# Attention pieces with two stacked parts, the key's exchanged form by transfers in SBUF, scores as two 32-row products a head

## Chip, cores and metric

One core of a Trainium2 chip runs the whole program in one launch. The metric is the device time of that launch in microseconds. Three runs of the kernel before were timed; a further execution was profiled.

## The reference

The program is one block of a network on 4 batches of 256 tokens with 512 features: attention with 32 heads of 16 features and a small adapter, a feed layer with a selection, a state-space mixer, and the feed layer again. Only the attention is touched. Cut to it:

```python
qkv = jnp.einsum('btc,oc->bto', x, w_attn)                 # x: (4, 256, 512), normed
q, k, v = split into heads: (4, 32, 256, 16)
q = _apply_rope(q, cos, sin); k = _apply_rope(k, cos, sin)
scores = jnp.einsum('bhqd,bhkd->bhqk', q, k) / sqrt(16)
scores = jnp.where(causal, scores, -inf)
y = jnp.einsum('bhqk,bhkd->bhqd', softmax(scores), v)
# adapter: 10 extra keys and values, the same for all batches
ascores = gating * softmax(jnp.einsum('bhqd,xhkd->bhqk', q, ak) / sqrt(512))
y = y + jnp.einsum('bhqk,xhkd->bhqd', ascores, av)
out = jnp.einsum('btc,oc->bto', y, w_proj)
```

## The kernel before

All numbers are float32. [...]

**Units.** The attention loop has 32 passes, i = 0 to 31; pass i handles four heads `u = i % 8` of batch `b = i // 8`. In what follows a pass is a unit. The order of TensorE's instructions in the loop is the order of the program (`manual_schedule` for that engine); the order on the other engines and queues is made by the framework's planner from its own cost estimates.

**Rows.** `prepared` makes for each batch and each half c of its 256 tokens the rotated queries (f = 0) and keys (f = 1), 128 tokens by 32 heads by 16 features, `qk[b, c, f]`. GpSimd adds the two halves of the rotation at L329.

**Pieces.** A piece covers eight heads, so two units: `pieces(b, q, f)`. `stacked` (L347, L348, GpSimd) writes each head's 16 features four times side by side, as upper and lower parts: for queries the parts stand as upper, upper, lower, nothing (cleared once at L338), for keys as upper, lower, upper. One cast writes the two upper copies (128x256), one subtraction the lower part (128x128). Then TensorE turns four blocks of 128 columns for each half c (L442, tile `trp`, two PSUM banks), and ScalarE copies each bank into the piece `pc0` or `pc1` (L444). Now a head stands in 64 rows, two heads to a block of 128 rows.

**When.** `pieces` runs in two steps: GpSimd's part at the end of unit i, TensorE's and ScalarE's part in unit i + 1. Queries are turned in even units, keys in odd ones; the unit after the keys' turn (an even one) is the first to use that piece of keys. The queries' piece is one unit earlier still. The first piece of queries and of keys is made before the loop.

**Scores.** `scores(b, u)` multiplies, for each half c of the queries, each of four heads' 64 rows by the keys' 64 rows (L488): for c = 1 against all 256 keys, for c = 0 against the first 128. Heads in rows 0 to 63 and 64 to 127 go to two PSUM banks, pool `a_s` with three. VectorE adds the causal mask and takes the maximum (L499), ScalarE takes the exponential (L511). The products for c = 1 stand at the start of a unit, those for c = 0 after the unit's long products (the projections `pq` of the next batch, `po` or the feed layer).

**The rest of a unit**, in TensorE's order: scores for c = 1; on even units `adapter_scores` (`pa`, L452, from a query piece and the adapter's keys `akbd`); the turn of a piece (`trp`); the long products; scores for c = 0; the weighted sums of the unit two before (`py`, L538 and L544); the turn of the exponentials of the unit before (`ptr`, L528, copied by ScalarE and VectorE at L529); the turn of the sums (`try`, L558); on even units the turn of the adapter's scores (`tra`, L460); sometimes turns of other tiles. All these PSUM tiles but scores and `py` share the pool `a_m` with four banks. In units 28 to 31 and behind the loop the feed layer's products `pd` use two of these banks at a time until VectorE and ScalarE have chosen from them.

**The adapter's keys.** `adapter_weights` multiplies the 10 extra keys, repeated eight times, and masks them (`bdk`) so that 20 rows hold two heads side by side; `adapter_keys` stacks and turns them into `akbd` (L378, L381), in unit 1.

**Loads.** `load` is a transfer issued by SyncE (SP). In the loop SP issues the projection's weights (L297, asked for in unit 3) and, from unit 23 on, the feed layer's (L199); both wait for GpSimd to free their buffers.

Of the kernel before, what the change touches and what calls it, by code (L numbers as in the profile page):

```python
# [9 lines left out]
F32 = mybir.dt.float32  # L10
F32R = mybir.dt.float32r
# [3 lines left out]
AF = mybir.ActivationFunctionType  # L15
ALU = mybir.AluOpType
# [4 lines left out]
P = 128  # L21
B, L, C = 4, 256, 512
# [4 lines left out]
NH, HD = 32, 16  # L27
NA = 10
# [11 lines left out]
COLS = {}  # L40
_at = 0
for _name, _w in (
    ("ident", 128), ("neg", 256), ("rot", 128), ("bdk", 2), ("bdv", 128), ("idx", 1), ("tri", 256),
):
    COLS[_name] = (_at, _at + _w)
    _at += _w
# [5 lines left out]
def constants():  # L52

    c = np.zeros((P, NCOL), np.float32)

    def put(name, v):
        c[: v.shape[0], COLS[name][0] : COLS[name][1]] = v

    r = np.arange(P)
    put("ident", np.eye(P, dtype=np.float32))  # L60
    put("tri", (np.arange(L)[None, :] >= r[:, None] % Q).astype(np.float32))
    put("neg", np.where(np.arange(L)[None, :] - P > r[:, None], -1e30, 0.0).astype(np.float32))
    theta = (
        np.float32(1.0)
        / np.float32(10000.0) ** (np.arange(0, HD, 2, dtype=np.float32) / np.float32(HD))
    ).astype(np.float32)
    angle = np.outer(np.arange(L, dtype=np.float32), theta).astype(np.float32)
    cos, sin = np.cos(angle), np.sin(angle)
    table = np.stack([np.concatenate([cos, cos], 1), np.concatenate([-sin, sin], 1)], 1)
    table = np.stack([table * np.float32(0.25), table], 1).astype(np.float32)  # L70

    put("rot", table.reshape(2, P, -1).transpose(1, 0, 2).reshape(P, -1))
    put("bdk", (r[:, None] // NA == np.arange(2)[None, :]).astype(np.float32))
    put("bdv", (np.arange(80)[:, None] // NA == r[None, :] // HD).astype(np.float32))
    put("idx", r[:, None].astype(np.float32))
    return c
# [3 lines left out]
def hybrid_kernel(  # L80
# [6 lines left out]
    nc = tc.nc  # L87
    load = nc.sync.dma_start
# [5 lines left out]
    con = keep.tile([P, NCOL_KEEP], F32R, name="con")  # L94
    ident = con.bitcast(F32)
# [3 lines left out]
    a_s = keep.tile([P, 1], F32, name="a_s")  # L99
# [172 lines left out]
    def attention(later, region):  # L272
        with ExitStack() as es:
            inner, banks = ExitStack(), ExitStack()
            pool = lambda name, bufs, **kw: es.enter_context(tc.tile_pool(name=name, bufs=bufs, **kw))
            w1 = pool("a_w", 1)
            p1 = pool("a1", 1)
            p2 = pool("a2", 2)
            p3 = pool("a3", 3)
            ps, ps_s, ps_y = (  # L280
                banks.enter_context(tc.tile_pool(name=name, bufs=bufs, space=PSUM))
                for name, bufs in (("a_m", 4), ("a_s", 3), ("a_y", 1))
            )

            acon = w1.tile([P, NCOL_ATTN - NCOL_KEEP], F32, name="acon")
# [46 lines left out]


            NS = 2
            stacks = [[w1.tile([P, 8, 4, HD], F32R, name=f"st{f}{i}") for i in range(NS)] for f in range(2)]
            for f in range(2):
                for v in stacks[f]:
                    nc.gpsimd.memset(v.bitcast(F32), 0.0)  # L338
            turn_at = [0, 0]
            HI = (slice(0, 2), slice(0, 3, 2))  # L340
            LO = (2, 1)

            def stacked(src, f, n=P):
                st = stacks[f][turn_at[f] % NS]
                turn_at[f] += 1
                v = src.unsqueeze(2)
                nc.gpsimd.tensor_copy(st[:n, :, HI[f], :], v.to_broadcast([n, 8, 2, HD]))  # L347
                nc.gpsimd.tensor_tensor(  # L348
                    st[:n, :, LO[f], :], src, st[:n, :, 0, :].bitcast(F32), ALU.subtract
                )  # L350
                return st.rearrange("p h s d -> p (h s d)")


            wte_s = p1.tile([P, 2, C], F32, name="wte_s", tag="ya")
# [2 lines left out]
            AW = 8 * NA  # L357
# [3 lines left out]
            def adapter_weights():  # L361
                pk = ps.tile([80, C], F32, name="pk", tag="m")
                mm3(pk, [[v[:, k, :] for v in wt] for k in range(KC)],
                    [[v[:, k, :] for v in wk_s] for k in range(KC)])
                ak = p2.tile([80, NH, HD], F32, name="ak", tag="t1")
                bdk = col("bdk")[:20].unsqueeze(1).unsqueeze(3).to_broadcast([20, NH // 2, 2, HD])
                nc.vector.tensor_tensor(
                    ak[:20].rearrange("p (b e) d -> p b e d", e=2),
                    pk[:20].rearrange("p (b e d) -> p b e d", e=2, d=HD), bdk, ALU.mult,
                )  # L370
                return ak

            def adapter_keys(ak):
                for q in range(4):
                    s = stacked(ak[:20, q * 8 : q * 8 + 8, :], 1, 20)
                    tr = ps.tile([P, 4, 2 * NA], F32, name="tra", tag="m")
                    for j in range(4):
                        nc.tensor.transpose(tr[:, j, :], s[:20, j * P : (j + 1) * P].bitcast(F32), ident[:20, :20])  # L378

                    o = akbd[:, 4 * q * AW : (4 * q + 5) * AW].rearrange("p (j w) -> p j w", j=4)  # L380
                    nc.scalar.copy(o[:, :, : 2 * NA], tr)  # L381

            avbd = w1.tile([80, 4, P], F32, name="avbd")

# [49 lines left out]
            def pieces(b, q, f):  # L434

                st = [stacked(qk[b, c, f][:, q * 8 : q * 8 + 8, :], f) for c in range(2)]
                yield
                o = p2.tile([P, 4, L], F32R, name=f"pc{f}", tag=f"pc{f}")
                for c in range(2):
                    tr = ps.tile([P, 4, P], F32R, name="trp", tag="m")  # L440
                    for j in range(4):
                        nc.tensor.transpose(tr[:, j, :], st[c][:, j * P : (j + 1) * P], con)  # L442
                    cs = slice(c * P, (c + 1) * P)
                    nc.scalar.copy(o[:, :, cs], tr)  # L444
                turned_.setdefault((b, q), []).append(o)
                yield

            def adapter_scores(b, q):
                pa = ps.tile([AW, L], F32, name="pa", tag="m")
                for j in range(4):  # L450
                    n = (4 * q + j) * AW
                    nc.tensor.matmul(  # L452
                        pa, akbd[:, n : n + AW], turned_[b, q][0][:, j, :], start=(j == 0), stop=(j == 3)
                    )
                sa = p2.tile([AW, 4, P], F32, name="sa", tag="paT").rearrange("p s i -> p (s i)")[:, :L]
                nc.scalar.copy(sa, pa)
# [18 lines left out]
            def scores(b, u):  # L475

                qT, kT = turned_[b, u // 2]
                es_ = [p2.tile([P, 4, (c + 1) * P], F32, name=f"e{c}", tag=f"e{c}") for c in range(2)]
                made, tops = [], []

                def products(c):
                    n = (c + 1) * P
                    pair = [ps_s.tile([P, 2, n], F32, name="sc", tag="sc") for _ in range(2)]
                    for j in range(2):
                        blk = (u % 2) * 2 + j
                        for pr in range(2):
                            rows = slice(64 * pr, 64 * pr + 64)
                            nc.tensor.matmul(  # L488
                                pair[pr][:, j, :], qT[rows, blk, c * P : (c + 1) * P],
                                kT[rows, blk, :n], start=(j == 0), stop=(j == 1),  # L490
                            )
                    for pr, sc in enumerate(pair):
                        made.append((c, pr))
                        reduced(c, pr, sc)

                def reduced(c, pr, sc):
                    nm = p3.tile([P, 2], F32, name="nmx", tag="nmx", bufs=4)
                    for j in range(2):
                        nc.vector.tensor_tensor_reduce(  # L499
                            es_[c][:, 2 * j + pr, :].rearrange("p (k i) -> p k i", i=P),  # L500
                            sc[:, j, :].rearrange("p (k i) -> p k i", i=P), mask[:, 1 - c :, :],
                            -1.0, 3e38, ALU.add, ALU.min, nm[:, j : j + 1],
                        )
                    tops.append(nm)

                for c in (1, 0):
                    products(c)
                    yield
                    for (c_, pr), nm in zip(made, tops):
                        for j in range(2) if c_ == c else ():  # L510
                            nc.scalar.activation(  # L511
                                es_[c][:, 2 * j + pr, :], es_[c][:, 2 * j + pr, :], AF.Exp, scale=-1.0,
                                bias=nm[:, j : j + 1],
                            )
                    if c:
                        yield
                all_es[8 * b + u] = es_
                yield

            def turn(es_):  # L520
                e0, e1 = (
# [159 lines left out]
            n = B * 8  # L681
# [32 lines left out]
            with tc.manual_schedule(engines={nc.tensor.engine}):  # L714
                for i in range(n):
# [21 lines left out]
                    next(scoring)  # L737
                    step("long", i)
                    step("values", i)
                    next(scoring)  # L740
                    if 2 <= i:
                        py = weigh(*divmod(i - 2, 8), eTs.pop(i - 2))
                    if 1 <= i:
# [1174 lines left out]
```

## Time and profile before

| | us |
|---|---|
| runs, median of three | 1805.07 |
| runs, lowest and highest | 1799.9, 1806.85 |
| the profiled execution | 1803.91 |
| its span in the trace | 1802.1 |
| mean granted TensorE clock | 0.993 of full |
| ACT: busy in the span | 1281.4 |
| transposes `trp` (L442): 256, mean of one | 0.256 |
| scores (L488): 128 of 256 columns, mean of one | 0.336 |
| scores (L488): 128 of 128 columns, mean of one | 0.305 |
| copies of pieces (L444): 64, mean of one | 0.587 |
| GpSimd's cast for the stacks (L347): 64, mean of one | 0.397 |

TensorE's instructions overlap: one starts before the one before it has ended. What an instruction costs is therefore read from the distance between starts, and a "busy" sum of several kinds can pass the span. The loop is entered at 33 us and left at about 297 us.

### The profile page before, as it was taken

What the parts mean: (1) busy time and instruction counts of PE and PEld (TensorE: products, weight loads), DVE (VectorE), ACT (ScalarE), POOL (GpSimd) and SP (SyncE); (2) the same over time, 40 slices, a digit from 0 to 9 for tenths busy, and PEclk for the clock granted to TensorE, in tenths of its full rate; (3) what the DMA queues carried; (4) which work ended last, traced back from release to release, by engine and by line L of the source; (5) the groups of instructions that cost most, each with busy time, mean ns of one, the idle gap of its engine ahead of it and who ended that gap; (6) DMA issues with size and microseconds to landing.
All of it is one profiled execution on the core that took longest, in us unless ns stands there. A gap on an engine that the chain in (4) does not pass through costs nothing.

```text
span 1802.1 us, 32962 instructions
## 1 busy us (share of the span) xinstructions
PE 1754.3 (97%) x12734; PEld 1427.0 (79%) x12734; DVE 1419.8 (79%) x2515; ACT 1281.4 (71%) x2321; POOL 251.2 (14%) x253
## 2 busy tenths in 40 slices
PE   8999989899999999999999999999999999999998
PEld 6777767678877888888888888888888888888877
DVE  5566677889998788787878797878787878887777
ACT  5677685578887668766866686768667867777754
POOL 6433230111110111011100101110111101101100
PEclk8999999999999999999999999999999999999999
DMA  4000000122344234323433252325333433343231
GB/s 145 8 1 1 23 14 26 43 73 98 108 128 137 80 106 153 120 85 98 154 100 100 88 160 88 111 81 176 103 97 105 142 106 94 112 141 112 88 97 57
DMA packets 134381, 169.51 MB, mean 94 GB/s; under 512 B 12240, under 2 KB 77520, under 8 KB 134224
## 3 DMA queue, kind: packets, MB, share of 16 engines
q1 hardware_dynamic: 125152, 134.37, 24.4%
q10 hardware_dynamic: 9072, 33.03, 4.9%
q8 instruction: 100, 1.64, 0.4%
q14 instruction: 57, 0.47, 0.1%
HBM read 131.71 MB, written 35.65 MB: 93 GB/s over the span
## 4 chain that ended last, share of the span: by engine, by line
PE 79%; DVE 10%; ACT 7%; issue 2%; POOL 1%; DMA 1%; SPq 0%; ACTq 0%; DVEq 0%; POOLq 0%
PE pp L115 14%; PE pp L117 13%; PE pp L116 13%; PE pyy L1258 8%; PE pog L115 6%; PE pog L116 6%; PE pog L117 6%; PE trx L1239 3%; ACT e L511 1%; DVE acc L986 1%; PE ptr L528 1%; PE pq L115 1%; PE pq L117 1%; PE trp L442 1%; PE pq L116 1%
## 5 line engine op out<-in xcount | busy, mean ns | idle before, releaser
L115 PE MATMUL pp<-mx,w 128*128 128x512 f32 x1144 | 459.6, 402 | 0.0
L117 PE MATMUL pp<-mx,w 128*128 128x512 f32 x1144 | 447.0, 391 | 0.0
L116 PE MATMUL pp<-mx,w 128*128 128x512 f32 x1144 | 446.4, 390 | 0.0
L1291 POOL TENSOR_TENSOR sq<-sq,x 128x1024 f32<-128x1024 f32 x54 | 132.1, 2446 | 1177.8 <-ACT x L1290 1177.8
L117 PEld LDWEIGHTS pp<-mx,w 128*128 128x128 f32 x1144 | 214.8, 188 | 46.1
L115 PEld LDWEIGHTS pp<-mx,w 128*128 128x128 f32 x1144 | 215.0, 188 | 44.6
L986 DVE SCALAR_TENSOR_TENSOR acc<-pp,cw_s,acc 128x1012 f32<-128x1012 f32 (+2 forms) x192 | 244.5, 1273 | 4.3
L116 PEld LDWEIGHTS pp<-mx,w 128*128 128x128 f32 x1144 | 215.3, 188 | 40.3
L1232 DVE TENSOR_TENSOR em<-em,gm 128x1280 f32<-128x1280 f32 x128 | 189.5, 1489 | 72.1 <-ACT em L1227 72.1
L115 PE MATMUL pog<-wo,gh 128*128 128x512 f32 x512 | 200.8, 392 | 1.9 <-DVE x L1387 1.9
L117 PE MATMUL pog<-wo,gh 128*128 128x512 f32 x512 | 199.8, 390 | 0.9 <-DVE gh L1370 0.9
L116 PE MATMUL pog<-wo,gh 128*128 128x512 f32 x512 | 199.5, 390 | 0.0
L1242 DVE TENSOR_TENSOR xd<-trx,dt_t 128x512 f32<-128x512 f32 x128 | 82.3, 685 | 141.5 <-PE trx L1239 141.5
L1158 ACT ACT_TABLE_LOAD x63 | 80.8, 1283 | 138.7 <-DVE acc L986 138.6
L1449 ACT ACTIVATE gt<-pp 128x1024 f32<-128x1024 f32 x64 | 65.6, 1025 | 145.2 <-PE pp L117 145.2
L1258 PEld LDWEIGHTS pyy<-em,xd 64*64 64x64 f32 x4096 | 130.3, 133 | 44.1 <-issue 17.6
L1219 ACT ACTIVATE em<-r,end_t 128x128 f32<-128x128 f32 x512 | 163.0, 389 | 0.8
L1258 PE MATMUL pyy<-em,xd 64*64 64x256 f32 (+3 forms) x4096 | 157.8, 300 | 3.2 <-DVE em L1232 3.0
L511 ACT ACTIVATE e<-e,nmx 128x256 f32<-128x256 f32 (+1 forms) x256 | 100.7, 453 | 42.3 <-DVE nmx L499 42.0
L115 PEld LDWEIGHTS pog<-wo,gh 128*128 128x128 f32 x512 | 96.1, 188 | 24.7 <-issue 2.7
L117 PEld LDWEIGHTS pog<-wo,gh 128*128 128x128 f32 x512 | 96.1, 188 | 22.1 <-DVE gh L1370 2.1
L116 PEld LDWEIGHTS pog<-wo,gh 128*128 128x128 f32 x512 | 96.2, 188 | 19.3
(323 smaller groups left out, 3141.0 us busy)
## 6 DMA issues: line engine op xcount, KB each, us to landing
wr<-in_win_dram SPq DMA_DIRECT2D x144, 256.0 KB, 2.8
r<-cumd SPq DMA_DIRECT2D x256, 128.0 KB, 2.9
spill<-gb ACTq DMA_DIRECT2D x63, 512.0 KB, 2.8
gr<-spill SPq DMA_DIRECT2D x120, 256.0 KB, 3.4
wor<-in_wout_dram SPq DMA_DIRECT2D x64, 256.0 KB, 4.7
out_dram<-x SPq DMA_DIRECT2D x7, 256.0 KB, 2.6
x<-in_x_dram SPq DMA_DIRECT2D x1, 1536.0 KB, 9.1
gr<-spill SPq DMA_DIRECT2D x8, 192.0 KB, 2.5
```

The lines of the kernel that those rows point to most:

```text
L115: nc.tensor.matmul(o, lh, rh, start=(first and k == 0), stop=False)
L116: nc.tensor.matmul(o, lh, rl, start=False, stop=False)
L117: nc.tensor.matmul(o, ll, rh, start=False, stop=(last and k == n - 1))
L511: nc.scalar.activation(es_[c][:, 2 * j + pr, :], es_[c][:, 2 * j + pr, :], AF.Exp, scale=-1.0, bias=nm[:, j : j + 1],)
L986: nc.vector.scalar_tensor_tensor(av[:, :, d:], pv[:, :, : L - d], cw_s[:, ch, tap : tap + 1], av[:, :, d:], ALU.mult, ALU.add,)
L1158: nc.scalar.activation(pair(x2).rearrange("p k u i -> p u k i"), acc.rearrange("p (u k i) -> p u k i", u=2, i=Q), AF.Silu,)
L1219: nc.scalar.activation(piece(e, j, c, 2 - c, 2), rv[:, j, 2:, :], AF.Exp, bias=end_t[:, 2 * j + c, h : h + 1],)
L1232: nc.vector.tensor_tensor(e, e, gm, ALU.mult)
L1242: nc.vector.tensor_tensor(xd[:, hs, :].rearrange("p c (h d) -> p c h d", h=2), tr.rearrange("p c (h d) -> p c h d", h=2), dt_t[:, hs, 2 * ...
L1258: nc.tensor.matmul(py[d, u, j * L + c * Q : (j + 1) * L].rearrange("p (k i) -> p k i", i=Q), xd[us, 4 * j + c, d], piece(es2[hh], j, c)[us ...
L1291: (nc.gpsimd if n < NB - 2 else nc.vector).tensor_tensor(sqs[g], sqs[g], x2, ALU.add)
L1449: nc.scalar.activation(gts[i], pp, AF.Silu)
```

## The change

A head's features are stacked in two parts (upper, lower), 32 rows, four heads to a block of 128 rows. A piece has two blocks, both halves c in one PSUM bank, so four turns and one copy in place of eight and two. The keys' piece gets a second copy in which each head's two parts are exchanged (lower, upper): `swapped` makes it by eight transfers inside SBUF, each of 16 partitions by 512 float32 (2 KB a partition), issued by SP. A head's scores are then two products of 32 rows: queries by keys (upper by upper plus lower by lower) and queries by exchanged keys (upper by lower plus lower by upper).

Both halves c of the scores now stand at the start of the unit, in one group of sixteen products: for c = 1 the four heads against the plain keys, then against the exchanged keys; then the same for c = 0. Each head has a PSUM bank for both halves. Pool `a_s` has four banks, `a_m` three. The exponentials follow in two steps.

The adapter's keys stand in 40 rows, four heads side by side; upper and lower parts are stacked in both orders, one by GpSimd and one by VectorE. The stacks are no longer cleared, since every column is written.

```diff
-                for name, bufs in (("a_m", 4), ("a_s", 3), ("a_y", 1))
+                for name, bufs in (("a_m", 3), ("a_s", 4), ("a_y", 1))
...
-            stacks = [[w1.tile([P, 8, 4, HD], F32R, name=f"st{f}{i}") for i in range(NS)] for f in range(2)]
-            for f in range(2):
-                for v in stacks[f]:
-                    nc.gpsimd.memset(v.bitcast(F32), 0.0)
+            stacks = [[w1.tile([P, 8, 2, HD], F32R, name=f"st{f}{i}") for i in range(NS)] for f in range(2)]
             turn_at = [0, 0]
-            def stacked(src, f, n=P):
+            def stacked(src, f, n=P, engine=nc.gpsimd, first=0):
                 st = stacks[f][turn_at[f] % NS]
                 turn_at[f] += 1
-                v = src.unsqueeze(2)
-                nc.gpsimd.tensor_copy(st[:n, :, HI[f], :], v.to_broadcast([n, 8, 2, HD]))
-                nc.gpsimd.tensor_tensor(
-                    st[:n, :, LO[f], :], src, st[:n, :, 0, :].bitcast(F32), ALU.subtract
-                )
+                upper, lower = st[:n, :, first, :], st[:n, :, 1 - first, :]
+                engine.tensor_copy(upper, src)
+                engine.tensor_tensor(lower, src, upper.bitcast(F32), ALU.subtract)
                 return st.rearrange("p h s d -> p (h s d)")
+
+            def swapped(dst, src):
+
+                for at in range(0, P, HD):
+                    load(dst[at : at + HD].bitcast(F32), src[at ^ HD : (at ^ HD) + HD].bitcast(F32))
...
             def adapter_keys(ak):
                 for q in range(4):
-                    s = stacked(ak[:20, q * 8 : q * 8 + 8, :], 1, 20)
-                    tr = ps.tile([P, 4, 2 * NA], F32, name="tra", tag="m")
-                    for j in range(4):
-                        nc.tensor.transpose(tr[:, j, :], s[:20, j * P : (j + 1) * P].bitcast(F32), ident[:20, :20])
+                    tr = ps.tile([P, 2, 2, 4 * NA], F32, name="tra", tag="m")
+                    for i, engine in enumerate((nc.gpsimd, nc.vector)):
+                        s = stacked(ak[:40, q * 8 : q * 8 + 8, :], 1, 40, engine, i).bitcast(F32)
+                        for j in range(2):
+                            nc.tensor.transpose(tr[:, i, j, :], s[:40, j * P : (j + 1) * P], ident[:40, :40])
...
-                o = p2.tile([P, 4, L], F32R, name=f"pc{f}", tag=f"pc{f}")
+                o = p2.tile([P, 1 + f, 2, L], F32R, name=f"pc{f}", tag=f"pc{f}")
+                tr = ps.tile([P, 2, L], F32R, name="trp", tag="m")
                 for c in range(2):
-                    tr = ps.tile([P, 4, P], F32R, name="trp", tag="m")
-                    for j in range(4):
-                        nc.tensor.transpose(tr[:, j, :], st[c][:, j * P : (j + 1) * P], con)
-                    cs = slice(c * P, (c + 1) * P)
-                    nc.scalar.copy(o[:, :, cs], tr)
+                    for j in range(2):
+                        nc.tensor.transpose(
+                            tr[:, j, c * P : (c + 1) * P], st[c][:, j * P : (j + 1) * P], con
+                        )
+                nc.scalar.copy(o[:, 0], tr)
+                if f:
+                    swapped(o[:, 1], o[:, 0])
...
+                banks_ = [ps_s.tile([P, 3, P], F32, name="sc", tag="sc") for _ in range(4)]
+                for c, at in ((1, slice(0, 2)), (0, slice(2, 3))):
                     n = (c + 1) * P
...
+                    for v in range(2):
+                        for r in range(4):
+                            rows = slice(32 * r, 32 * r + 32)
                             nc.tensor.matmul(
-                                pair[pr][:, j, :], qT[rows, blk, c * P : (c + 1) * P],
-                                kT[rows, blk, :n], start=(j == 0), stop=(j == 1),
+                                banks_[r][:, at, :].rearrange("p k i -> p (k i)"),
+                                qT[rows, 0, u % 2, c * P : (c + 1) * P], kT[rows, v, u % 2, :n],
+                                start=(v == 0), stop=(v == 1),
                             )
...
@@ loop over the units @@
                     step("values", i)
-                    next(scoring)
                     if 2 <= i:
```

## The prediction

> **What bounds the kernel now.** I read four views in this order: the page's busy times, a table of stages, the order of time of TensorE in two units of the attention loop, and the transfers. The first two say where the change can act. "Unit" is one pass i of the 32-pass loop (four heads of one batch); a unit's start is its first product of scores with 256 columns.
>
> ```profile
> PE 1754.3 (97%) x12734; PEld 1427.0 (79%) x12734; DVE 1419.8 (79%) x2515; ACT 1281.4 (71%) x2321; POOL 251.2 (14%) x253
> 180.00:220.00 40.00, 39.37 (x323) 30.43 (x323) 26.07 (x119) 28.80 (x73) 13.59 (x26) 1.00 0.09 26
> 220.00:260.00 40.00, 35.60 (x322) 27.21 (x321) 27.86 (x129) 34.64 (x82) 16.34 (x26) 0.96 0.06 17
> ```
>
> The attention loop runs from 33 to about 297 us of a span of 1802.1; all that follows is untouched. In the loop TensorE is busy 39.4 of 40 us, so a shorter TensorE stream shortens the time; only around 220 to 260 us does ScalarE (34.6 of 40) set the pace.
>
> ```profile
> 64.78 0.50 PE L488 MATMUL sc<-pc,pc 64*128 64x256 f32 x4
> 65.21 0.89 PE L442 MATMUL trp<-con,st 128*128 128x128 f32 x8
> 65.94 0.47 PE L115 MATMUL pq<-wk,axs 128*128 128x512 f32 x1
> ...
> 68.90 0.44 PE L488 MATMUL sc<-pc,pc 64*128 64x128 f32 x4
> 69.27 0.64 PE L538 MATMUL py<-eT,av 128*32 128x256 f32 x8
> ...
> 71.74 0.50 PE L488 MATMUL sc<-pc,pc 64*128 64x256 f32 x4
> ```
>
> Starts are what counts here, since durations overlap. Scores with 256 columns hold TensorE from 64.78 to 65.21 (0.43), those with 128 columns from 68.90 to 69.27 (0.37), eight transposes of pieces from 65.21 to 65.94 (0.73; in the next unit, 72.70 to 73.34, 0.64; so 0.086 each). The unit takes 71.74 - 64.78 = 6.96. Followed so through the loop, odd units last 6.84 to 6.96 (units 3, 5, 7, 13, 15, 21, 27), 7.33 to 7.98 (11, 19, 23, 25, 29) and 10.0 to 10.3 (9, 17).
>
> ```profile
> 143.08 0.73 PEld L442 LDWEIGHTS trp<-con,st 128*128 128x128 f32 x8
> 143.65 1.08 ACT L444 CAST pc<-trp 128x512 fp32r<-128x512 f32 x2
> 1.64 1.85 SPq L300 DMA_DIRECT2D ar<-in_wq_dram  x4
> 197.63 0.55 SPq L187 DMA_DIRECT2D fi<-in_cst_dram  x1
> 198.23 0.58 SPq L189 DMA_DIRECT2D fa<-in_asg_dram  x1
> nw_s<-in_nw_dram SPq DMA_DIRECT2D x1, 32.0 KB, 1.7
> cumd<-dc SPq DMA_DIRECT2D x2, 256.0 KB, 2.0
> r<-cumd SPq DMA_DIRECT2D x256, 128.0 KB, 2.9
> 33.27 0.50 PEld L488 LDWEIGHTS sc<-pc,pc 64*128 64x128 f32 x4 [0.86 <-ACT pc L444]
> PEld tra L460 <- ACT eT L529: 3.7, 11, 0.6
> ```
>
> These price the new path: a copy of pieces starts 0.57 after its transposes' first load; SP needs 0.47 from one issue to the next with 128 partitions (four in 1.85, the last 0.43), and 0.60 (197.63 to 198.23) with 64; small transfers land 1.7 to 2.9 after issue.
>
> **Removed.** Transposes of pieces fall from 256 to 128: 128 x 0.086 = 11.0 us of TensorE. Scores: 0.80 a unit in two groups becomes one group of sixteen 32-row products. Before, two 64-row products start together and the next pair's load begins 0.11 later (four loads span 0.30 = 0.11 + 0.19). If four 32-row products go side by side, the group is a load 0.11, two rounds of 256 columns at 0.11, one 128-column round held up by the next load 0.11, one of 0.05, and the 0.10 before another kind of product can load: 0.59. That is 0.21 less, 32 times, 6.7 us. If only two go side by side, eight rounds bound by loads give 0.11 + 8 x 0.11 + 0.10 = 1.09, and 32 x 0.29 = 9.2 us are lost. I take the first: the weighted sums at L538, on four strips of columns, issue eight products in 0.46.
>
> [...]
>
> Together 17.7 us of TensorE, 0.55 a unit. Where another engine sets the pace (units 24 to 27) it isn't paid out: 17.7 x 28/32 = **-15.5 us**. One copy of 0.59 fewer a unit on ScalarE, half the elements in GpSimd's cast and no cleared stacks count nothing, being under TensorE; were ScalarE bound throughout, they would be the gain instead. The adapter's keys (units 0 and 1) get eight castings shared by GpSimd and VectorE in place of four pairs on GpSimd: nothing, bounds -1 and +1.
>
> **Added: the exchange.** For each of 16 key pieces SP issues eight transfers of 16 partitions, 32 KB each. The keys' pieces are transposed in odd units and read at the start of the next. In an odd unit: scores to 0.59, first transpose load there, copy from 1.16 to 1.75, SP starts at 1.82. The eighth issue is seven steps later, 7 x 0.47 = 3.3 to 7 x 0.62 = 4.3 (0.60, and 0.69 from fa to the next issue, are the 64-partition steps); I take 3.8, between, since 16 partitions are fewer descriptors but shaped like the slower rows. Landing: 1.7 to 2.9, I take 1.9, nearest to the row of 32 KB. So the exchanged half is there at 7.5 (bounds 6.8 and 9.0). The next unit wants it 0.11 after its start, in a unit of 6.95 at 6.95 - 0.55 + 0.11 = 6.5. TensorE stalls 1.0, in order, with everything of that unit behind it. Seven units of 6.95: 7.0; 11, 19, 23: 0.5 each; 25: 0.2. **+8.7 us** (bounds: 7 x 0.3 = 2, and 7 x 2.5 + 3 x 2.0 + 1.7 + 1.5 = 27). Nothing else on SP in this stretch waits long except the loads at L297 and L199, which stand behind GpSimd; one of them ahead of an exchange would cost up to its own wait, once or twice.
>
> [...] No transfer inside SBUF is in this trace.
>
> **Start.** Unit 0 has no slack: its scores start at 33.27, as soon as the copy ends. With GpSimd's four casts before it some 0.15 shorter each, the copy ends at 32.6, and the exchange lands at 32.6 + 0.07 + 3.8 + 1.9 = 38.4: 5.1 later. Back come waits of units 0 and 1 for VectorE and GpSimd that have time to finish meanwhile, 0.91 + 0.89 + 0.55 = 2.3; unit 1, short of work, adds 0.5 for its own exchange. **+3.3 us** (bounds +2.1 and +6.6).
>
> **Banks.** The shared PSUM buffers go from 4 to 3, with one fewer use a unit (one trp for two). The transposes tra already wait 0.34 each for a bank that eT leaves; a pair pd holds two of three in the feed units. I take **+3 us**, bounds 0 and +8. VectorE's reductions of both halves now follow the whole group, 0.2 later, with the unit to do it in: nothing; if VectorE were late, the four score banks would be, and the next unit with them.
>
> **Sum.** -15.5 + 8.7 + 3.3 + 3 = -0.5 on the profiled execution of 1803.91 (span 1802.1), which stands 1.2 below the runs' median of 1805.07. Forecast: about **1804 us, no change** that can be told (0.5% is 9 us). Own range 1796 to 1813.
>
> **Rivals.** (1) The exchange is nearly hidden: steps of 0.47 and 1.7 to land, -15.5 + 2 + 2.1 + 0.5 = -11, **1794**. For it: issue steps of all 128-partition rows. Against: seven units have under 4.8 us left after the copy. Chance 0.26. (2) Slower: the exchange takes the place of the removed work as what each second unit waits for. With steps of 0.62 and 2.9 to land, -15.5 + 27 + 5 + 2 = +18, **1823**. It decides from an arrival at about 8.2 on, where stalls pass 16 us. For it: 64-partition issues and r's 2.9; against: those read DRAM. Chance 0.28. (3) Four strips don't run side by side: 16 us more, **1820**; against it the pairs at L488. Chance 0.06. The forecast keeps 0.40.
>
> **Numbers.** Faster 0.26, same 0.40, slower 0.34. The range 1790 to 1824 takes in rival 1 and most of 2 and 3; beyond it lie the upper bounds of several terms at once.
>
> **What would show it.** 128 trp transposes at 0.086; sixteen sc products in about 0.6; SP's step between the eight issues and the landing of pc<-pc; a wait of sc for that DMA in even units, about 1 us, and about 5 us near 33 us; tra's waits for eT. I am wrong if even units don't wait, if scores take over 0.8, or if another engine's waits appear in the feed units.

## The result, and the profile after

The changed kernel takes 1857.78 us (median of four runs, 1857.26 to 1861.13) against 1803.9 before: 1.0311 times as long, 95% interval 1.0294 to 1.0329. The forecast was 1804, with a range of 1790 to 1824. The profiled execution shown here took 1861.13 us, span 1859.3.

The page's first lines, and the table of windows over the attention loop (columns: length, then busy us and instructions of PE, PEld, DVE, ACT and POOL, the granted clock, the DMA share, GB/s):

```profile
span 1859.3 us, 33408 instructions
...
PE 1779.4 (96%) x12862; PEld 1440.4 (77%) x12862; DVE 1428.7 (77%) x2523; ACT 1270.9 (68%) x2293; POOL 240.6 (13%) x249
```

```profile
60.00:340.00 280.00, 246.86 (x2005) 188.10 (x2005) 162.97 (x694) 166.74 (x404) 66.45 (x129) 0.89 0.08 20
...
180.00:220.00 40.00, 35.81 (x309) 27.36 (x309) 25.52 (x103) 22.96 (x55) 9.31 (x19) 0.91 0.06 14
220.00:260.00 40.00, 36.20 (x265) 27.62 (x267) 20.03 (x92) 21.67 (x54) 9.58 (x21) 0.87 0.16 39
```

In 180 to 220 us TensorE was busy 39.4 of 40 before; now it is 35.8, and at 0.91 of its granted clock instead of 1.00. All engines have become idler: that is the picture of a wait, not of another engine that has become the bound. Where it sits, TensorE's order of time in one odd and one even unit shows:

```profile
70.57 0.68 PE L493 MATMUL sc<-pc,pc 32*128 32x256 f32 x16
71.18 0.55 PE L445 MATMUL trp<-con,st 128*128 128x128 f32 x4
71.56 0.47 PE L115 MATMUL pq<-wk,axs 128*128 128x512 f32 x1
...
77.01 0.50 PE L493 MATMUL sc<-pc,pc 32*128 32x256 f32 x5
77.72 0.35 PE L493 MATMUL sc<-pc,pc 32*128 32x256 f32 x1 [0.20 <-DMA pc<-pc]
78.99 0.35 PE L493 MATMUL sc<-pc,pc 32*128 32x256 f32 x1 [0.92 <-DMA pc<-pc]
80.24 0.52 PE L493 MATMUL sc<-pc,pc 32*128 32x256 f32 x9 [0.90 <-DMA pc<-pc]
80.69 0.70 PE L458 MATMUL pa<-pc,akbd 128*80 128x256 f32 x4
```

The odd unit's sixteen products hold TensorE from 70.57 to 71.18, 0.61 us; its four transposes from there to 71.56, 0.38. The even unit's sixteen need 80.69 - 77.01 = 3.68: five run at once, four against the plain keys and one against the exchanged, and then the first product of each of the other three strips (32 rows, one head) waits for its own transfers. What made them late stands in the order of time of VectorE, ScalarE and SP's queue in the odd unit:

```profile
70.68 0.55 DVE L158 TENSOR_SCALAR axn<-x,amv,ars 128x512 f32<-128x512 f32 x1 [1.08 <-PE tr L166]
71.29 0.69 DVE L108 TENSOR_TENSOR axs<-tr,axs 128x512 fp32r<-128x512 f32 x1
71.90 0.41 DVE L501 CUSTOM_DVE_ANT_0 e<-sc,acon 128x256 f32<-128x256 f32 x1
...
72.42 0.91 ACT L509 ACTIVATE e<-e,nmx 128x256 f32<-128x256 f32 x2 [1.16 <-DVE nmx L501]
73.23 0.56 ACT L448 CAST pc<-trp 128x512 fp32r<-128x512 f32 x1
...
73.82 4.94 SPq L349 DMA_DIRECT2D pc<-pc  x8
```

The keys' copy begins at 73.23, 2.66 after the unit's start: on ScalarE it stands behind two exponentials that wait 1.16 for VectorE. In the fifteen odd units with such a copy it begins 2.0 to 2.7 us after the start, and in three of them (7, 15, 23) 4.1 to 5.1. SP takes 4.94 for eight issues, 0.62 from one to the next. The transfers' row and the sum of the waits:

```profile
pc<-pc SPq DMA_DIRECT2D x128, 32.0 KB, 1.9
```

```profile
PEld sc L493 <- DMA pc<-pc: 31.0, 30, 2.2
PE sc L493 <- DMA pc<-pc: 26.6, 35, 2.0
```

(Loads and products wait at the same time; the two are not added.)

### The profile page after: what moved, and what is told of

It reads as the page before. It is cut to its first block, busy times and chain, and to the rows that moved or that the text cites. A ratio compares the mean times of both kernels' runs of the same rounds, so it can differ in the third digit from the quotient of the medians.

```text
span 1859.3 us, 33408 instructions
## 1 busy us (share of the span) xinstructions
PE 1779.4 (96%) x12862; PEld 1440.4 (77%) x12862; DVE 1428.7 (77%) x2523; ACT 1270.9 (68%) x2293; POOL 240.6 (13%) x249
## 4 chain that ended last, share of the span: by engine, by line
PE 76%; DVE 9%; ACT 5%; SPq 3%; DMA 2%; issue 2%; POOL 1%; ACTq 0%; DVEq 0%; POOLq 0%
PE pp L115 13%; PE pp L117 13%; PE pp L116 13%; PE pyy L1253 7%; PE pog L115 6%; PE pog L116 6%; PE pog L117 6%; SPq L349 3%; PE trx L1234 3%; DMA pc<-pc 1%; DVE acc L981 1%; ACT e L509 1%; PE ptr L524 1%; PE pg L1171 1%; PE pq L115 1%
```

## The experiments

Each ratio is against the kernel before on the same chip (medians 1802.88 for the first four, 1800.37 for the next four, 1803.76 for the ninth and tenth, 1800.28 for the last two). Where sums are made below, differences of ratios times 1803 us are used.

**1. No exchange at all.** The transfers are left out, and the second round of products reads the plain keys again.

```diff
-                if f:
-                    swapped(o[:, 1], o[:, 0])
...
-                                ... kT[rows, v, u % 2, :n],
+                                ... kT[rows, 0, u % 2, :n],
```

> Leaves out the eight transfers a piece; both products of a head read the plain keys, so the lower-by-upper terms of the scores are missing. Theory L (the exchange comes too late, and nothing else is wrong): the waits of even units go, the clock stays whole, and the time is the profile before less 15 us plus at most 3 for the banks: 1788 to 1793. Rival F (the new form itself, sixteen 32-row products in one group, reductions in a block, three banks, is slow): most of the 54 us stays, 1830 or more.

Measured: 1804.13 us, 1.0003 (0.9994 to 1.0013). A miss, and the first surprise: without any exchange the change still gains nothing. Its loop starts unit 31 at 279.65 us, the kernel before at 286.8, so 7 us were gained by then; they are lost in unit 31 and behind it. TensorE's order of time in unit 31:

```profile
284.44 0.66 PE L522 MATMUL ptr<-con,e 128*128 128x128 f32 x4
286.70 0.65 PE L522 MATMUL ptr<-con,e 128*128 128x128 f32 x4 [1.60 <-DVE fx L248]
287.62 1.08 PE L522 MATMUL ptr<-con,e 128*128 128x128 f32 x4 [0.27 <-DVE fx L248]
...
290.42 0.44 PE L115 MATMUL pd<-fw,axs 128*128 128x288 f32 x1
290.66 0.44 PE L116 MATMUL pd<-fw,axs 128*128 128x288 f32 x1
```

The feed layer's pair `pd` holds two of the three banks, so `ptr` waits 1.6 us for VectorE to leave one; behind the wait the feed products stand 0.24 apart. In the kernel before `ptr`'s twelve transposes run through there without a wait, the same products stand 0.13 to 0.14 apart, and the second weighted sums `py` come 9.9 us after the unit's start instead of 15.5.

**2. Exchange issued, but not read.** Only the second line of the edit above: all 128 transfers run, and nobody waits for them.

> Issues the eight transfers a piece as the changed kernel does, but no product reads what they write; the scores read the plain keys twice. Theory L: what costs is the wait alone, so within 2 us of the kernel without transfers. Rival T (their traffic, or SP's queue being held 5 us per piece, delays other loads and engines): 5 to 30 us above it.

Measured: 1803.25 us, 1.0006 (0.9994 to 1.0017). As expected: the transfers, their traffic and SP's time cost nothing that can be told by themselves (the ratio is 0.0003 above run 1's, well inside the intervals). Reading them costs 1.0311 - 1.0006, 55 us.

**3. Three banks in the kernel before.**

```diff
-                for name, bufs in (("a_m", 4), ("a_s", 3), ("a_y", 1))
+                for name, bufs in (("a_m", 3), ("a_s", 3), ("a_y", 1))
```

> The kernel before with three shared PSUM banks instead of four, nothing else. The prediction's term: +3 us (0 to 8), so 1804 to 1812, here with one more use of a bank per unit than the changed kernel has. Rival F in the form 'the fourth bank is what is missing': +20 us or more, 1824 up.

Measured: 1822.11 us, 1.0098 (1.0074 to 1.0122): 18 us for one bank, where the prediction had +3 and at most +8, and the rival +20 or more. A row of its waits that the kernel before does not have:

```profile
PEld try L558 <- ACT eT L529: 14.6, 27, 1.6
```

The small transposes `try` wait for ScalarE's copy of `eT` in 27 of 32 units, since the three tiles of `ptr` fill all three banks.

**4. Keys a unit earlier.** The keys' pieces are turned in even units, the queries' in odd ones, so that the exchange has a whole unit more.

```diff
...
-            part = pieces(0, 1, 0)
+            part = pieces(0, 1, 1)
...
-                        part = pieces(b, u // 2, (i + 1) % 2)
+                        part = pieces(b, u // 2, i % 2)
```

> The changed kernel with keys' pieces turned in even units and queries' in odd ones: the same work, all transfers read, and one unit (some 7 us) more between an exchange and its reader; the first piece of keys, before the loop, is as before. Theory L: waits for pc<-pc vanish but at 33 us; without them 1790, with 5 us at the start 1793 to 1799. Rival F or T: still above 1820, since nothing but the time of the exchange is changed.

Measured: 1811.58 us, 1.0051 (1.0034 to 1.0068). 47 of the 55 us are back: units 4 to 22 have the lengths of run 1. The number is still 13 us above what was expected. What is left is the start, where unit 0 still takes 14.93 us against 9.21 in run 1 and units 1 and 2 are 1.0 longer each, and 2.5 us in units 23 to 25.

**5. Four transfers instead of eight.** Each exchanges neighbouring blocks of 32 rows; the bytes are the same.

```diff
-                for at in range(0, P, HD):
-                    load(dst[at : at + HD].bitcast(F32), src[at ^ HD : (at ^ HD) + HD].bitcast(F32))
+                for at in range(0, P, 2 * HD):
+                    frm = at ^ (2 * HD)
+                    load(dst[at : at + 2 * HD].bitcast(F32), src[frm : frm + 2 * HD].bitcast(F32))
```

> The exchange as four transfers of 32 partitions in place of eight of 16, the same bytes; blocks of 32 rows change places, so a head's second product meets another head's keys (the scores are not the reference's). Theory L, that SP's step of 0.63 from issue to issue is the bulk: the last lands 2.5 us sooner, a wait of some 3 us in even units falls under 1, and the clock keeps whole in most of them: 1810 to 1826. Rival: bytes, or the time one transfer takes to land, set it: 1850 or more.

Measured: 1815.09 us, 1.0076 (1.0059 to 1.0092), as expected. SP's queue and the transfers' row:

```profile
72.73 2.41 SPq L350 DMA_DIRECT2D pc<-pc  x4
pc<-pc SPq DMA_DIRECT2D x64, 64.0 KB, 2.0
```

A step between issues is still 0.63 us and the landing 2.0 us, with twice the partitions in each. So it is the number of issues, not the bytes: four steps less, 2.5 us an exchange, give back 42 us.

**6. No exchange, four shared banks.** Run 1, and `py` moved from a bank of its own into the shared pool, so that it takes turns with all the others there in four banks; the scores keep the other four.

```diff
-                for name, bufs in (("a_m", 3), ("a_s", 4), ("a_y", 1))
+                for name, bufs in (("a_m", 4), ("a_s", 4))
...
-                py = ps_y.tile([P, L], F32, name="py", tag="py")
+                py = ps.tile([P, L], F32, name="py", tag="m")
```

> The run without exchange (plain keys read twice, no transfers), with py's sums in the shared PSUM pool and that pool back at four banks; scores keep their four, py's own bank goes. Theory: the missing 15 us of that run are the bank's, as the kernel before with three banks says (+18): 1785 to 1791. Rival: TensorE's shorter stream is worth nothing because VectorE or ScalarE sets the pace: 1800 to 1805.

Measured: 1794.96 us, 0.9964 (0.9952 to 0.9976). The profiled execution has a span of 1788.1, 14 less than before, inside what was expected; the median misses it and is only 6.5 less. That execution was the fastest of the six, at a granted clock of 0.993; the other five had 0.988 to 0.990 over the whole span. No trace of one of those was kept, so where they lose 5 us isn't known. Against run 1 the fourth bank is worth 0.0039, 7 us. In unit 31 the wait at `ptr` is 1.31 us instead of 1.60 and 0.27, the second `py` come 11.2 us after the unit's start instead of 15.5, and the feed products stay 0.13 apart.

**7. TensorE kept busy in the wait.** Twenty products of constants into a free corner of a score bank, ahead of each even unit's scores.

```diff
+                for _ in range(20 if u % 2 == 0 else 0):
+                    nc.tensor.matmul(banks_[3][:, 2, :], con, con, start=True, stop=True)
```

> The changed kernel with 20 products of the identity with itself ahead of the scores of even units, into a score bank that is overwritten; 20 x 0.11 = 2.2 us of TensorE in a stretch in which it would wait some 3 us. Theory L with the clock as its second half (after a wait TensorE runs at half clock for 3.4 to 6.8 us): some 1 to 1.5 us come back in each of 15 units, 1835 to 1845. Rival (the wait alone, the clock costs little): 1856 or more.

Measured: 1858.19 us, 1.0312 (1.0298 to 1.0327). The number expected of a clock effect is missed, and the rival's (1856 or more) is met; but the trace does not bear the rival's reason out. TensorE's order of time, its waits, and its window row:

```profile
80.47 2.43 PE L489 MATMUL sc<-con 128*128 128x128 f32 x20
82.83 0.50 PE L495 MATMUL sc<-pc,pc 32*128 32x256 f32 x7
83.87 0.53 PE L495 MATMUL sc<-pc,pc 32*128 32x256 f32 x9 [0.54 <-DMA pc<-pc]
84.33 0.70 PE L458 MATMUL pa<-pc,akbd 128*80 128x256 f32 x4
```

```profile
PE sc L495 <- DMA pc<-pc: 6.4, 10, 0.9
```

```profile
60.00:340.00 280.00, 261.60 (x2344) 210.71 (x2344) 169.71 (x724) 170.12 (x416) 67.54 (x130) 0.96 0.08 20
```

The twenty products delay the scores by 2.36 us, 38 us in sixteen units, and take the place of waits. The wait row (26.6 in the changed kernel, 6.4 here) counts only TensorE's idle time ahead of products; counted by how long the even units' sixteen products hold TensorE beyond run 1's, the stalls fall from 42 us to 12. That alone would make the kernel 8 us slower; it isn't, and of the two profiled executions this one is even 5.5 us the faster (1855.58 against 1861.13). The clock over the loop rises from 0.89 to 0.96 of full. Taken over the stretches below full clock, TensorE's busy time times the missing share of the clock falls from 27.3 us to 12.0, 15 less. The rival had taken the twenty products for free, and so had the theory; that the clock accounts for the balance is read from these rows, not tried by itself.

**8. Early keys, four shared banks, first key piece turned in both orders.** The early keys of run 4 and the four shared banks of run 6, with all transfers read; for the first key piece of all, where nothing can be earlier, GpSimd and VectorE write both orders of the parts, and TensorE turns both.

```diff
...
+                turns = f == 1 and (b, q) == (0, 0)
...
+                for v in range(2 if turns else 1):
...
-                if f:
+                if f and not turns:
                     swapped(o[:, 1], o[:, 0])
```

> The changed kernel mended: keys turned one unit earlier, the first piece of keys exchanged by turning a second stack (upper and lower in the other order, by GpSimd and VectorE) in place of transfers, and four shared banks as in the run without exchange. Theory: all three costs gone, 1786 to 1793, faster than both kernels. Rival: with the exchange read in time some other cost of it (SP, the DMA engines) stays: 1800 or more.

Measured: 1800.31 us, 0.9991 (0.9979 to 1.0004). Nothing on TensorE waits for an exchange any more, and yet it is 7 us more than hoped, a number in the rival's range. Units 24 and 25 hold that much, 12.69 and 9.89 us against 9.46 and 5.94 in run 6. SP's queue, TensorE and ScalarE there:

```profile
199.94 15.88 SPq L362 DMA_DIRECT2D pc<-pc  x12
215.86 0.58 SPq L185 DMA_DIRECT2D fb<-in_ffb_dram  x1
...
217.71 10.66 SPq L199 DMA_DIRECT2D fr<-in_ffw_dram  x4
```

```profile
228.05 0.66 PE L542 MATMUL ptr<-con,e 128*128 128x128 f32 x4
232.18 1.97 PE L542 MATMUL ptr<-con,e 128*128 128x128 f32 x8 [3.47 <-ACT sa L481]
```

```profile
229.38 0.67 ACT L107 CAST fw<-fr 128x576 fp32r<-128x576 f32 x1 [1.09 <-DMA fr<-in_ffw_dram]
...
231.78 0.35 ACT L481 COPY sa<-pa 80x256 f32<-80x256 f32 x1
```

The row of twelve is the end of one exchange and the whole of the next, which stands at the head of SP's queue until its copy ends at 210.9 us (210.28 and 0.58 in ScalarE's order of time); the feed layer's loads stand behind it. In run 6 the loads `fr` begin at 194.09. So some other cost of the exchange does stay, as the rival had it: SP's queue. A late weight tile makes ScalarE's cast wait 1.09 us, in order, with everything behind it (the copy `sa` comes at 231.78); TensorE waits 3.47 us for a bank, and then takes 1.97 for eight transposes that take 1.09 in run 9.

**9. A second piece turned.** As run 8, and the key piece of unit 22 is turned in both orders too, so that SP has no exchange to wait for ahead of the feed layer's loads.

```diff
-                turns = f == 1 and (b, q) == (0, 0)
+                turns = f == 1 and (b, q) in ((0, 0), (3, 0))
```

> As the early keys with four banks, but a second key piece, the one made in unit 22, gets its exchanged form by being turned (four more transposes, one more copy) instead of by transfers. Theory of the blocked queue: in the run with early keys the exchange of unit 22 stands on SyncE's queue from 200 to 216 us until its copy comes, and the loads of the feed part behind it (bias, indices, four weight tiles) start at 216 instead of 195 us; the cast of such a tile on ScalarE waits for its landing at 228 us, the copies behind the cast are late, and TensorE waits 3.5 us in unit 24 and runs on at half clock. Without that exchange the loads start near 205 us, unit 24 takes 9.5 us instead of 12.7 and unit 25 about 6 instead of 9.9, and the kernel takes 1793 to 1796 us, 0.995 to 0.998 of before. Rival, the order itself is what costs there (scores of the adapter and two table loads in the same unit, whatever the queue does): unit 24 and 25 stay at 12 and 9 us and the time stays at 1799 to 1802 us.

Measured: 1797.09 us, 0.9962 (0.9951 to 0.9973): 7 us faster than the kernel before. SP's queue and TensorE's order of time:

```profile
201.65 0.53 SPq L185 DMA_DIRECT2D fb<-in_ffb_dram  x1
...
203.49 17.24 SPq L199 DMA_DIRECT2D fr<-in_ffw_dram  x4
```

```profile
231.49 1.09 PE L542 MATMUL ptr<-con,e 128*128 128x128 f32 x8 [1.81 <-ACT sa L481]
```

The loads start 14 us earlier, ScalarE's cast waits no longer, TensorE's wait falls from 3.47 to 1.81, and the eight transposes behind it take 1.09 instead of 1.97. Unit 24 takes 10.32 us and unit 25 8.86: about half of what the blocked queue was held to cost came back there. In unit 25 the granted clock averages 0.56 after that wait, where in run 6 it is whole (0.87 against 0.96 over 220 to 260 us); whether the order of the work brings the rest about, as the rival has it, was not tried. The time is 1 us above what was expected; the ratio is inside it.

**10. Turned throughout.** No transfers: both orders of the parts for every key piece, keys in odd units, four shared banks (the scores have the other four).

```diff
-                turns = f == 1 and (b, q) in ((0, 0), (3, 0))
+                turns = f == 1
...
-                        part = pieces(b, u // 2, i % 2)
+                        part = pieces(b, u // 2, (i + 1) % 2)
```

> No transfers at all: GpSimd writes both orders of the two parts for every key piece, TensorE turns both, ScalarE copies both; keys stay in odd units, and all seven banks that are not the scores' serve four buffers of the shared tag. Theory: nothing waits for an exchange, so the time is that of the run without exchange and with four banks (1795 us) plus 16 times the four added transposes (0.38 us from start to start), 6 us: 1799 to 1803 us, 0.998 to 1.002 of before, and unit lengths of odd units 0.4 us above that run's. Rival: GpSimd, which now writes twice as much for each key piece, or ScalarE with one more copy of 0.56 us ahead of the exponentials, comes late: the score products or the transposes wait in the units of the keys, 1806 us or more.

Measured: 1801.29 us, 0.9989 (0.9976 to 1.0002), as expected: odd units in the middle of the loop are 0.34 to 0.59 us longer than in run 6, but for 9 and 17, which are as long, and no new wait shows.

**11. The keys' transposes ahead of the scores.** The changed kernel with one step moved in odd units.

```diff
+                    if u % 2 and part:
+                        next(part)
+                        part = None
                     scoring = scores(b, u)
                     next(scoring)
```

> The changed kernel with one step moved: in odd units the four transposes of the keys' piece stand ahead of the unit's scores instead of behind them, so that their copy comes ahead of the exponentials on ScalarE. Nothing else differs. Theory: the wait in even units is set by the time of that copy, which the prediction put at 1.16 to 1.75 us after the unit's start and the trace has at 2.66 to 3.2. The copy then ends about 1.35 us after the unit's start and the eight issues begin about 1.9 us earlier than in the changed kernel; with the 43 us that 2.5 us less of issuing gave back, that is worth 33 us, and the kernel takes 1820 to 1832 us. Rival, the eight issues and their landings are the price whenever they start, because the queue or the landing is slow: the time stays at 1845 us or above.

Measured: 1835.78 us, 1.0201 (1.0181 to 1.0220). 20 of the 55 us are back, where 26 to 38 were expected: a miss by 4 us, and the rival's 1845 is 9 off. ScalarE and SP in the same odd unit:

```profile
69.93 0.59 ACT L448 CAST pc<-trp 128x512 fp32r<-128x512 f32 x1
71.19 2.88 ACT L509 ACTIVATE e<-e,nmx 128x256 f32<-128x256 f32 x8 [0.67 <-DVE nmx L501]
...
70.54 6.10 SPq L349 DMA_DIRECT2D pc<-pc  x8
```

The copy now begins 0.30 after the scores' start (69.63), and the issues at 0.91 instead of 3.25. But the eight take 6.10 us here instead of 4.94: in half of the sixteen exchanges one issue took 1.1 to 1.9 us instead of 0.59. In the changed kernel's trace a single issue does (1.25). What slows such an issue stays open.

**12. The copy later.** VectorE makes the keys' copy, behind its reductions.

```diff
-                nc.scalar.copy(o[:, 0], tr)
+                if f:
+                    nc.vector.tensor_copy(o[:, 0], tr)
+                else:
+                    nc.scalar.copy(o[:, 0], tr)
```

> The same step moved the other way: the copy of the keys' piece is made by VectorE, behind its eight reductions of the scores, instead of by ScalarE between the exponentials. It then ends about 4.3 us after the unit's start instead of 3.2. Theory, each microsecond by which the copy is later costs the stall and the half clock behind it in most of fifteen key units: 1.1 us later costs 14 to 22 us, 1871 to 1880 us. Rival, the copy's time is not what the even units wait for: 1858 us, or less for what ScalarE is spared.

Measured: 1871.43 us, 1.0395 (1.0375 to 1.0415). In the unit looked at, the copy ends 4.24 us after the scores' start instead of 3.22 (L449 below is the copy on VectorE): 1.0 us later, and the kernel is 14 to 15 us slower, at the lower edge of what was expected.

```profile
72.41 0.69 DVE L449 CAST pc<-trp 128x512 fp32r<-128x512 f32 x1
73.12 4.93 SPq L349 DMA_DIRECT2D pc<-pc  x8
```

## Why the prediction was wrong, point by point

**TensorE's gain: right in each unit, too large in the sum.** The sixteen products take 0.61 us (0.59 predicted), a transpose 0.095 (0.086), and units 3, 5, 13 and 21 of run 1 are 0.44 to 0.54 us shorter than before. With 0.61 against the 1.09 that was worked out for two at a time (an estimate from the loads' 0.11), four strips do run side by side; rival 3 falls. Paid out were 6.5 us (4.3 to 8.7) in run 6, not 15.5; its profiled execution shows 14.0 against that of the kernel before, and is 10.5 below the median of the kernel before on its own chip.

**The exchange: the step that failed.** The prediction had the exchanged half at 7.5 us after the odd unit's start, at most 9.0, against a want at 6.5, and priced that at +8.7, at most 27. Reading the exchange cost 55 us, of which about 6 are the start, so 49 against 8.7. Term by term, for the unit at 70.57:

- "copy from 1.16 to 1.75": it ran from 2.66 to 3.22. This is the first error. The working took the copy as free to begin 0.57 after its transposes, from a row in which the copies followed their transposes at once, and never placed it in ScalarE's order. There two exponentials stand ahead, which wait for VectorE, which begins its reductions only at 71.90, behind two steps of the norm (L158, L108). Runs 11 and 12 move this time, both ways, and the kernel follows. From the first issue to the even unit's scores there are 77.01 - 73.82 = 3.2 us in the changed kernel, 5.2 in run 11 and 2.2 in run 12: 2.0 us more gave 20 us (in that unit 1.2 of the 2.0 went into slower issues), 1.0 us less cost 14 to 15.
- "I take 3.8" for seven steps, from steps of 0.54: measured 0.62, 4.35, the upper end, and 16 partitions a transfer were not told from 32 (0.63 in run 5). That run also prices the count of issues: four fewer gave 42 us, more than the early copy of run 11 did.
- Landing 1.9: right.
- Together: the exchanged half is there at 3.25 + 4.35 + 1.9 = 9.5, and the stall is 3.68 - 0.61 = 3.1 us, three times what was predicted. Over the even units from 4 to 30 the stalls add up to 36 us, where eleven of them were priced at 8.7.
- The price of a stalled microsecond was wrong as well. Each stall was counted once. In the trace ten of the even units from the fourth on are 3.8 to 6.3 us longer than in run 1, 4.7 in the mean, for stalls of 2.3 to 4.8, 3.1 in the mean. TensorE's granted clock falls with the waits: 0.89 over the loop, against 0.98 in run 1.

```profile
60.00:340.00 280.00, 258.40 (x2310) 202.90 (x2309) 200.68 (x812) 183.47 (x445) 70.53 (x133) 0.98 0.05 16
```

That is run 1. From unit 0 to unit 31 the changed kernel's trace takes 58 us longer than run 1's. 42 of them are stalls (36 in the even units, 6 in unit 0). The other 16 come after the stalls, in work that takes longer. In 60 to 340 us the clock stands below full for 59.7 us in the changed kernel and 13.7 in run 1, and TensorE's busy time in these stretches times the missing share of the clock is 27.3 us against 6.6: 21 us more, enough for the 16. That the clock is all of it was not tried by itself.

The price shows in run 11 too. There the exchanged half lands 7.0 to 8.7 us after the odd unit's start, 7.6 in the median, which is what the prediction had; and yet 1.0201 - 1.0006, 35 us, remain: some 6 of them at the start, while the even units' stalls add up to only 14 in that run. Part of the rest belongs to the moved order (the even units 8, 10 and 18, without a stall there, are 1.0 to 1.3 us longer than in run 1), for which there is no run without exchange.

**The start.** +3.3 predicted. Unit 0 takes 15.42 us against 9.21 without the exchange, and unit 1 is 0.3 shorter: 5.9, inside the bounds. The waits that were to come back did not.

**The banks.** +3 predicted, bounds 0 and +8. The same bank costs the kernel before 18 us (run 3), and the changed one 7 (run 6 against run 1, where `py` moves in with the others). The rows that were read, `tra`'s waits, were not the ones that counted: `try` behind three tiles of `ptr`, and `ptr` behind the pair `pd`.

**The sum with measured terms:** -6.5 + 7 + 55 = +55.5, against a measured 1.0311, +56. It closes by construction, since each term is the difference between two of these kernels (run 6 and the kernel before, run 1 and run 6, the changed kernel and run 2), and so it is no check of the terms. Of the rivals, the second had the right mechanism, the exchange as what each second unit waits for, and a third of its size; of its two reasons the steps of 0.62 held, and the 2.9 to land did not.

## What to carry to other kernels

A step that is handed to another queue is late by what stands ahead of it in the order of each engine on its way (here the copy began 2.66 us after the unit's start, not 1.16); take the time at which its source is ready from that engine's own order in the stage at hand, not from a row in which the engine was free. A wait on TensorE is to be priced with the work that follows it at a lower clock (here 4.7 us for a stall of 3.1), and an exchange through SP by its number of issues (here 0.62 us each). When a bank is given up, ask who holds several of the shared banks at once, not who waits for one now; and when a queue gets a waiting transfer, ask which prefetch stands behind it.

## What was not expected of the hardware

Transfers inside SBUF with 16 or with 32 partitions each hold SP's queue 0.62 and 0.63 us, more than the 0.47 of four loads from DRAM with 128 partitions in the trace before (`in_wq_dram`, 1.64 to 3.49 us), though they move less. Half the issues with the same bytes were worth 42 us, while the landing stayed at 1.9 to 2.0: the cost was met on the issuing queue.

TensorE's granted clock fell to half after short waits. In run 1, waits of 1.60 and 0.27 us were followed by this window:

```profile
284.20:287.60 3.40, 1.55 (x20) 0.89 (x13) 3.18 (x20) 3.26 (x11) 0.65 (x1) 1.00 0.04 10
287.60:294.40 6.80, 6.37 (x26) 5.99 (x27) 3.94 (x13) 0.99 (x3) 0.64 (x1) 0.50 0.00 0
294.40:297.80 3.40, 3.27 (x36) 2.46 (x34) 2.67 (x7) 0.92 (x2) 0.00 (x0) 0.99 0.00 0
```

TensorE is busy 1.55 of 3.40 us, with no wait above 1.6 us, and then 6.8 us pass at 0.50 of the clock although it is busy 6.37 of them. In the changed kernel's trace the clock falls to 0.50 fifteen times between 30 and 400 us, for 3.4 to 10.2 us each; in the 3.4 us ahead of each fall TensorE was busy for 1.05 to 2.27 us. In the kernel before, TensorE runs nothing but transposes from 297.78 to 301.19 us, 2.74 us busy, and the clock stays whole there (1.00).
